# Last image of a four-layer network: layer 3's weights and position tables requested earlier, layer 2 in six PSUM banks, its result kept in SBUF

## The chip, the cores and the metric

The kernel runs on one core of one Trainium2 chip as one program for four images. The metric is device microseconds of that core. TensorE (PE) multiplies matrices, and its weight loads are listed apart (PEld); VectorE (DVE), ScalarE (ACT) and GpSimd (POOL) compute; SyncE (SP) issues nearly all DMAs, one after the other. Each engine takes its instructions in a fixed order: one that waits holds up all behind it.

## What is computed

The input is 4 images of 64x64 pixels (4096 tokens) with 128 channels, in float32. Each image passes through four layers:

```python
x = input + out_proj(norm(selective_scan(conv(in_proj(LN(input))))) * silu(z))   # layer 0
x = x + mlp(LN(x))
x = gamma * softmax_attention_over_all_tokens(x) + x                            # layer 1
y = hs(bn(conv1x1(x)))                                                          # layer 2, hs = hard swish
for m in range(2):
    y = y + hs(bn(conv3x3(hs(bn(conv1x1(y))))))
x = hs(bn(conv1x1(leaky(bn(concat(conv1x1(y), conv1x1(x)))))))
x = x + proj(softmax(q @ k + bias, over a 7x7 neighbourhood) @ v)               # layer 3, of LN(x)
x = x + mlp(LN(x))
```

In layer 3 a query sees 49 keys, and each of four heads adds a learned bias that depends on the offset between query and key.

## The kernel before

**Stages.** The selective scan of layer 0 takes most of the span: GpSimd, VectorE and ScalarE work on it without a break for images 0, 1, 2, 3 in turn. The rest of an image, `rest` (L1668), runs beside the next image's scan: `scan_output` (L581, layer 0's gate, projection and MLP), `layer1` (L731), `layer2` (L917) and `layer3_attention` (L1252). A tile scheduler orders each engine's instructions by priorities and estimated times, puts in the semaphore waits, and gives SBUF and PSUM space to pools as they open and close. A pool that takes space which another has held waits for that pool's last reader. So a load written early in the code can be issued only when its space is free, and one that is written late can be issued early.

The last image (3) has no scan beside it. For it `rest` is called with `scan_over` (L1747), which closes the scan's pools and so frees their SBUF, and the flag `wide` gives some stages larger tiles and more banks. When the scan ends, image 2's layer 3 is still at work; then comes image 3's `scan_output`, which steps image 2's last MLP beside it, and then layers 1, 2 and 3 of image 3.

**Tokens** are worked on in 8 chunks of 512 (8 rows). `transposed` keeps the image as xT, 128 channels by 4096 tokens, in SBUF from `scan_output` to the end of layer 2.

**Layer 2** first loads 15 small weights (`load`, through `loader`, L163, and L937 to L942); `norms` has the scales and shifts that the first activation (L956) reads. Then four kinds of phase follow: cv1 for all chunks; twice (m = 0, 1) the 1x1 convolutions of all chunks into `sides` tiles (two per step, with rows shifted by one for the next phase), and the 3x3 convolutions, twelve matmuls per chunk; at the end, chunk by chunk, cv3, cv2p and cv4 (L1003 to L1024). `hard_swish` (L952) is two activations on ACT and one or two operations on DVE. All PSUM tiles come from one pool of one-bank tiles, 8 for the last image and 4 for the others. The result `out_r` (L1021) of each chunk is stored to DRAM (x4).

**Layer 3.** `layer3_attention` loads its weights (12 loads for the last image, with those of the MLP), makes a bias row with a small matmul, and then works on chunks. `make_chunk` (L1328) loads the 512 tokens of a chunk from x4, normalizes and transposes them (`layernorm_T`, L178) and makes q, k and v, one chunk ahead of use. A chunk's keys are packed in four groups. `scores` (L1347) makes a group's scores, on the last image for all four heads at once (128x2048), takes the exp on ACT (L1361, tile e) and multiplies it on DVE by the exp of the bias (L1363). `products` (L1396) adds up the values and the denominators; `finish` (L1379) divides, projects and adds the residual, and on the last image queues the chunk's MLP, of which one step runs after each of the groups 1 to 3 of later chunks.

**Tables.** The biases lie in DRAM as tables by kind: 0 for chunk 0, 1 for chunks 1 to 6, 2 for chunk 7, four groups each. On the last image a table is 128x4x512 float32, 1 MB, loaded at its first use (`table`, L1318) and turned into its exp by ACT in place (L1324); twelve buffers hold all twelve. On images 0 to 2 tables are half as large, 8 buffers, and TensorE adds them to the scores (L1351) with no exp of their own.

Of the kernel before, what the change touches and what calls it, by code (L numbers as in the profile page):

```python
# [28 lines left out]
F32 = mybir.dt.float32  # L29
# [3 lines left out]
PSUM = bass.MemoryType.PSUM  # L33
# [880 lines left out]
    nc.sync.dma_start(D.w2_bias, last[0:1, 1, :])  # L914


def layer2(tc, K, A, D, img, xT, wide):  # L917

# [1 line left out]
    with ExitStack() as ctx:  # L922
        big = ctx.enter_context(tc.tile_pool(name="l2_big", bufs=1))
        pool = ctx.enter_context(tc.tile_pool(name="l2_w", bufs=2))
        psum = ctx.enter_context(tc.tile_pool(name="l2_ps", bufs=8 if wide else 4, space=PSUM))
        load = loader(tc, big, A, 2)
        cv1, cv2p = load("cv1_w", [128, 64]), load("cv2p_w", [128, 64])
        cv3 = big.tile([128, 64], F32, name="w2_cv3")
# [74 lines left out]
        for c in range(NCH):  # L1003
            i = c // (NCH // 2)
            half = slice(64 * i, 64 * i + 64)
            first = 1 + RC * c - i * (H - HALF)
            ps = psum.tile([128, LC], F32, name="ps")
            nc.tensor.matmul(ps[0:64, :], cv3[half, :], flat(y[half, first : first + RC, :]), start=True, stop=True)
            nc.tensor.matmul(ps[64:128, :], cv2p, xT[:, span(c)], start=True, stop=True)
            t = pool.tile([128, LC], F32, name="cat")  # L1010
            nc.scalar.activation(t, ps, AF.Identity, bias=norms[:, 5, 1:2], scale=norms[:, 5, 0:1])
            nc.scalar.activation(ps, ps, AF.Identity, bias=norms[:, 5, 1:2], scale=norms[:, 5, 0:1])
            nc.vector.scalar_tensor_tensor(t, t, 0.1, ps, ALU.mult, ALU.max)
            po = psum.tile([128, 4, 128], F32, name="ps")
            nc.tensor.matmul(
                po.rearrange("p t c -> p (t c)"), K.ones[0:1, :], bias.rearrange("p t c -> p (t c)"),
                start=True, stop=False,
            )
            for q in range(4):
                nc.tensor.matmul(po[:, q, :], t[:, span(q, 128)], cv4, start=False, stop=(q == 3))  # L1020
            r = pool.tile([128, 4, 128], F32, name="out_r")  # L1021
            nc.scalar.activation(r, po, AF.Relu, bias=K.half, scale=1.0 / 6.0)
            nc.vector.scalar_tensor_tensor(r, r, 1.0, po, ALU.min, ALU.mult)
            nc.sync.dma_start(token_tiles(D.x4[img], c), r)  # L1024

# [221 lines left out]
                nc.sync.dma_start(out[key_kind(c)][i], bt.rearrange("p h r w -> p h (r w)"))  # L1249


def layer3_attention(tc, K, A, D, img, wide, out=None):  # L1252

    nc = tc.nc
    NP = 4 if wide else 2
    with ExitStack() as ctx:  # L1260
        wpool = ctx.enter_context(tc.tile_pool(name="l3_w", bufs=1))
        pool = ctx.enter_context(tc.tile_pool(name="l3", bufs=2))
        psum = ctx.enter_context(tc.tile_pool(name="l3_p", bufs=1, space=PSUM))
        load = loader(tc, wpool, A, 3)
        n_w, n_b = load("norm1_g", [128, 1]), load("norm1_b", [128, 1])
        qkv, qkv_b, proj = load("qkv_w", [128, 3 * C]), load("qkv_b", [128, 3]), load("proj_w", [128, C])
        proj_b = load("proj_b", [1, C])
        qb = wpool.tile([128, 1], F32, name="qb")
        nc.vector.tensor_scalar_mul(qb, qkv_b[:, 0:1], HD**-0.5)


        made_in = ctx.enter_context(tc.tile_pool(name="l3_pm", bufs=1, space=PSUM)) if wide else psum

        def fresh(shape):
            return made_in.tile(list(shape), F32, name="fresh", tag="ps")


        pb = fresh((1, C))
        nc.tensor.matmul(pb, qkv_b[:, 2:3], proj, start=True, stop=True)
        bias = wpool.tile([1, 4, C], F32, name="bias_row")  # L1280
        nc.vector.tensor_add(bias, mid(pb, 4), mid(proj_b, 4))
        xs, qs, ks, vs, tables = {}, {}, {}, {}, {}
        mlps = []
        if wide:
            n2_w, n2_b = load("norm2_g", [128, 1]), load("norm2_b", [128, 1])
            P, together = load_mlp(load), Together(tc, K)

        def mlp_steps(c, x):
            xnT = pool.tile([128, LC], F32, name="xnT2", bufs=1)
            layernorm_T(tc, K, pool, made_in, x, n2_w, n2_b, xnT)  # L1290
            yield
            hT = pool.tile([128, NF, LC], F32, name="mlp_h", bufs=1)
            ph = psum.tile([128, NF, LC], F32, name="pair", tag="ps")
            for f in range(NF):
                mm = nc.tensor.matmul(ph[:, f, :], P.w1[:, span(f, 128)], xnT, start=True, stop=True)  # L1295
                if f == 0:
                    together.open(mm)
            together.run(
                mm,
                [  # L1300
                    lambda f=f: nc.scalar.activation(hT[:, f, :], ph[:, f, :], AF.Gelu, bias=P.b1[:, f : f + 1])  # L1301
                    for f in range(NF)
                ],
            )
            yield
            po = fresh((128, LC))
            for f in range(NF):
                nc.tensor.matmul(po, P.w2[:, f, :], hT[:, f, :], start=(f == 0), stop=(f == NF - 1))  # L1308
            yT = pool.tile([128, LC], F32, name="yT", bufs=1)
            nc.scalar.activation(yT, po, AF.Identity, bias=P.b2)  # L1310
            pt = fresh((128, 4, 128))
            for t in range(4):
                nc.tensor.transpose(pt[:, t, :], yT[:, span(t, 128)], K.ident)  # L1313
            nc.vector.tensor_add(x, x, pt)  # L1314
            nc.sync.dma_start(token_tiles(out, c), x)
            yield

        def table(c, i, p):  # L1318
            kind = key_kind(c)
            if (kind, i, p) not in tables:  # L1320
                t = pool.tile([128, NP, LC], F32, name="table", bufs=12 if wide else 8)
                nc.sync.dma_start(t, D.biasT[kind][i][:, NP * p : NP * p + NP, :])
                if wide:
                    nc.scalar.activation(t, t, AF.Exp)  # L1324
                tables[kind, i, p] = t
            return tables[kind, i, p]

        def make_chunk(c):  # L1328
            x = pool.tile([128, 4, 128], F32, name="x", bufs=6 if wide else 2)
            nc.sync.dma_start(x, token_tiles(D.x4[img], c))  # L1330
            xs[c] = x
            xn = pool.tile([128, LC], F32, name="xnT", bufs=1)
            layernorm_T(tc, K, pool, made_in, x, n_w, n_b, xn)
            ps = fresh((128, 2, LC))
            for i in range(2):
                nc.tensor.matmul(ps[:, i, :], qkv[:, span(i, C)], xn, start=True, stop=True)
            qs[c] = pool.tile([128, LC], F32, name="q")
            nc.scalar.activation(qs[c], ps[:, 0, :], AF.Identity, bias=qb, scale=HD**-0.5)
            ks[c] = pool.tile([128, LC], F32, name="k", bufs=3)
            nc.scalar.activation(ks[c], ps[:, 1, :], AF.Identity, bias=qkv_b[:, 1:2])  # L1340
            ps = fresh((128, 4, 128))
            for t in range(4):
                nc.tensor.matmul(ps[:, t, :], xn[:, span(t, 128)], qkv[:, 2 * C :], start=True, stop=True)
            vs[c] = pool.tile([128, 4, 128], F32, name="v", bufs=3)
            nc.scalar.copy(vs[c], ps)

        def scores(c, i, p, group):  # L1347
            ps, t = psum.tile([128, NP, LC], F32, name="pair", tag="ps"), table(c, i, p)
            if not wide:
                for u in range(NP):  # L1350
                    nc.tensor.matmul(ps[:, u, :], K.ident, t[:, u, :], start=True, stop=False)  # L1351
# [11 lines left out]
                made = nc.vector.tensor_mul(e, e, t)  # L1363
            return [e[:, u, :] for u in range(NP)], made

        row = bias.rearrange("p t c -> p (t c)")

        def product(out, tile_, q0, q1, at, values, es, made, last):
            for h in range(HEADS):
# [9 lines left out]
        def finish(c, po, den):  # L1379
# [5 lines left out]
            pj = psum.tile([128, 4, 128], F32, name="pj", tag="den")  # L1385
            nc.tensor.matmul(pj.rearrange("p t c -> p (t c)"), K.ones[0:1, :], row, start=True, stop=False)
            for t in range(4):
                nc.tensor.matmul(pj[:, t, :], oT[:, span(t, 128)], proj, start=False, stop=(t == 3))
            x = xs.pop(c)
            nc.vector.tensor_add(x, x, pj)  # L1390
            if wide:
# [276 lines left out]
def rest(tc, K, A, D, img, last, scan_over=None, out=None):  # L1668


    wide = scan_over is not None
    with ExitStack() as ctx:
        xT = transposed(ctx, tc)
        scan_output(tc, K, A, D, img, xT, last, scan_over)
        layer1(tc, K, A, D, img, xT, wide)
        layer2(tc, K, A, D, img, xT, wide)
    layer3_attention(tc, K, A, D, img, wide, out)


def everything_again(tc, K, A, D, out):  # L1680
# [3 lines left out]
    for img in range(B):  # L1684
        with ExitStack() as ctx:
            S = make_scan(ctx, tc, K, A)
            scan_inputs(tc, K, A, D, img)
            selective_scan(tc, K, S, D, img)
        with ExitStack() as ctx:
            xT = transposed(ctx, tc)  # L1690
            scan_output(tc, K, A, D, img, xT, None)
            layer1(tc, K, A, D, img, xT, False)
            layer2(tc, K, A, D, img, xT, False)
        layer3_shifted(tc, K, A, D, img)
        layer3_mlp_alone(tc, K, A, D, img, out[img], 4)

# [135 lines left out]
```

## Time and profile before

| | us |
|---|---|
| median of 4 runs (8837.91 to 8844.23) | 8842.63 |
| the profiled execution | 8850.58 |
| its span, first to last instruction | 8848.8 |
| scan's end, last y_sum (ACT) | 7656 |
| image 3: first matmuls of layer 1 | 8044.6 |
| layer 1's last update of xT (DVE, end) | 8425.2 |
| first layer-2 weight load issued; `norms` issued; first activation (L956) | 8420.8; 8429.7; 8431.6 |
| last out_r activation of layer 2 | 8529.0 |
| layer 3: weight loads issued (12) | 8529.1 to 8534.7 |
| layer 3: tables issued (12) | 8536.2 to 8561.6 |
| layer 3: first exp of scores; the next | 8573.6; 8579.6 |

Busy shares over the span: PE 80%, DVE 81%, ACT 64%, POOL 80%. The profile cuts the span in 40 slices of 221 us and gives each engine's busy share in tenths; the last image's layers fill the slices from 36 on. A windows view gives, for any stretch, each engine's busy time with its instruction count, the TensorE clock that was granted (PEclk, 1.00 is full speed), the share of the DMA engines' time and the rate in GB/s. A timeline view lists one engine's instructions: start, duration, operation and tiles, and in brackets the idle time before and what ended it.

### The profile page before, as it was taken

To read this page: it belongs to the slowest core of one execution; us is meant where nothing else is said; L and a number is where in the kernel's file an instruction comes from. 1 tells how busy PE (TensorE), PEld (TensorE's weight loads), DVE (VectorE), ACT (ScalarE), POOL (GpSimd) and SP (SyncE) were. 2 spreads that over 40 slices of the span, in tenths; PEclk is the share of its full clock that TensorE was granted. 3 is DMA by queue.
4 is the path that set the end of the run, shared out by engine and by line. 5 is a ranking of instruction groups with operands and counts; after the bars stand their busy time and mean duration, and the time that the engine had idled before them with its cause. 6 is when DMAs were issued, how large, how long until landed. Compare 5 with 4: busy or idle time off the path is not lost. (4 is left out here: it accounts for less than half of the span.)

```text
span 8848.8 us, 102218 instructions
## 1 busy us (share of the span) xinstructions
PE 7045.3 (80%) x30532; PEld 2633.4 (30%) x30532; DVE 7136.6 (81%) x8531; ACT 5686.2 (64%) x11661; POOL 7046.6 (80%) x3079
## 2 busy tenths in 40 slices
PE   6845858687788888787789888777799987788988
PEld 2211313132332222233322222334322222344333
DVE  4788978787999999997899999988899999513433
ACT  5646767676676676666766676667766676454356
POOL 6888999989899998997799999998899989500000
PEclk8756868797789998888899998888899988899989
DMA  5777676777545456565454556665455565320020
GB/s 186 243 231 242 238 252 239 261 242 266 192 162 170 168 173 216 194 210 185 164 168 166 182 168 227 201 216 182 157 173 172 176 214 196 107 71 6 1 81 12
DMA packets 855474, 1572.03 MB, mean 178 GB/s; under 512 B 218341, under 2 KB 336764, under 8 KB 851197
## 3 DMA queue, kind: packets, MB, share of 16 engines
q1 hardware_dynamic: 724605, 1389.21, 47.2%
q10 hardware_dynamic: 130304, 176.19, 5.6%
q8 instruction: 245, 4.01, 0.2%
q14 instruction: 320, 2.62, 0.1%
HBM read 1273.92 MB, written 280.18 MB: 176 GB/s over the span
## 5 line engine op out<-in xcount | busy, mean ns | idle before, releaser
L501 POOL TENSOR_TENSOR dB<-du,b_rows 128x1024 f32<-128x1024 f32 x2048 | 4813.7, 2384 | 490.4 <-issue 127.9
L507 ACT ACTIVATE dA<-dt,w_A_log 128x512 f32<-128x512 f32 x4096 | 2781.7, 690 | 504.9 <-DVE hc L509 239.8
L509 DVE TENSOR_TENSOR_SCAN dA<-dA,state,dB 128x512 f32<-128x512 f32 x2128 | 2631.6, 1273 | 275.0 <-POOL dB L501 139.3
L522 POOL TENSOR_TENSOR hc<-hc,c_rows 128x1024 f32<-128x1024 f32 x832 | 1984.4, 2385 | 46.0 <-ACT state L518 21.5
L509 DVE TENSOR_TENSOR_SCAN hc<-dA,state,dB 128x512 f32<-128x512 f32 x1456 | 1801.9, 1268 | 186.3 <-ACT dA L507 106.3
L514 DVE TENSOR_TENSOR hc<-dA,c_rows 128x512 f32<-128x512 f32 x2432 | 1564.8, 676 | 79.1 <-PE py L555 64.3
L555 PE MATMUL py<-hc,pick 128*32 128x512 f32 x8192 | 1251.3, 685 | 403.7 <-POOL hc L522 310.1
L516 ACT COPY state<-dA 128x1 f32<-128x1 f32 x2128 | 326.7, 159 | 1299.5 <-DVE hc L514 1292.8
L845 PE MATMUL pa<-e,l_v 128*128 128x512 f32 x2048 | 1062.0, 650 | 26.5 <-ACT e L801 25.2
L797 PE MATMUL pair<-l_g,l_f 32*128 32x512 f32 x2048 | 529.3, 663 | 163.9 <-ACT e L801 119.9
L801 ACT ACTIVATE e<-pair 128x1024 f32<-128x1024 f32 (+1 forms) x448 | 508.4, 1135 | 232.1 <-PE pair L797 224.2
L985 POOL MEMSET l_h<- 64x128 f32 x8 | 1.7, 212 | 815.0 <-DVE l_h L959 815.0
L845 PEld LDWEIGHTS pa<-e,l_v 128*128 128x128 f32 x2048 | 374.6, 199 | 677.9 <-issue 615.1
L555 PEld LDWEIGHTS py<-hc,pick 128*32 128x32 f32 x8192 | 210.3, 116 | 1171.8 <-POOL hc L522 461.7
L247 PE MATMUL ps<-band,w_conv_diag 128*128 128x504 f32 (+3 forms) x1152 | 500.8, 594 | 7.6 <-ACT delta L397 7.2
L1351 PE MATMUL pair<-table,ident 128*128 128x512 f32 x768 | 405.6, 653 | 103.9 <-ACT e L1361 79.9
L509 DVE TENSOR_TENSOR_SCAN dA<-dA,dB 128x512 f32<-128x512 f32 x304 | 356.2, 1213 | 63.5 <-POOL dB L501 55.3
L201 PE MATMUL ps<-ident,ln_xn 128*128 128x128 f32 x512 | 143.6, 374 | 307.4 <-ACT ln_xn L198 239.4
L328 POOL TENSOR_TENSOR du<-delta,xc 128x1024 f32<-128x1024 f32 x128 | 332.7, 2606 | 53.4 <-ACT delta L397 46.7
L1361 ACT ACTIVATE e<-pair 128x1024 f32<-128x1024 f32 (+1 forms) x224 | 254.7, 1137 | 174.5 <-PE pair L1355 174.2
L247 PEld LDWEIGHTS ps<-band,w_conv_diag 128*128 128x128 f32 x1152 | 221.4, 193 | 285.5 <-issue 264.5
L797 PEld LDWEIGHTS pair<-l_g,l_f 32*128 32x128 f32 x2048 | 139.6, 188 | 517.7 <-ACT e L801 255.5
(285 smaller groups left out, 8739.8 us busy)
## 6 DMA issues: line engine op xcount, KB each, us to landing
b_rows<-bc_dram SPq DMA_DIRECT2D x1024, 256.0 KB
c_rows<-bc_dram SPq DMA_DIRECT2D x1024, 256.0 KB
dt<-delta_dram SPq DMA_DIRECT2D x512, 512.0 KB
du<-du_dram SPq DMA_DIRECT2D x512, 512.0 KB
delta_dram<-delta ACTq DMA_DIRECT2D x128, 512.0 KB
du_dram<-du SPq DMA_DIRECT2D x128, 512.0 KB
table<-biasT_dram SPq DMA_DIRECT2D x72, 512.0 KB
y_first_dram<-y_sum ACTq DMA_DIRECT2D x128, 256.0 KB
```

Of the source, the lines that this page charges most:

```text
L247: mm = nc.tensor.matmul(out[:, r0 - row0 : r1 - row0, c0:c1], lhsT((dy + 1) * 3 + dx + 1), src[:, r0 + dy : r1 + dy, c0 + dx : c1 + dx], s ...
L328: nc.gpsimd.tensor_mul(du.rearrange("p d (a b) -> p d a b", b=H), deltas[b].rearrange("p d (a b) -> p d a b", b=H), tk,)
L501: nc.gpsimd.tensor_mul(dB, dus[pp], mid(bt, 2))
L507: nc.scalar.activation(dA, dts[pp][:, g, :], AF.Exp, scale=S.A[:, k, j, pr, g : g + 1])
L509: nc.vector.tensor_tensor_scan(hg[:, order], dA[:, order], dB[:, g, order], 0.0 if i == 0 else state[:, j, pr, g : g + 1], ALU.mult, ALU.add,)
L514: mm = nc.vector.tensor_mul(hc[:, g, :], dA, ct)
L522: made.append(nc.gpsimd.tensor_mul(hc, hc, mid(ct, 2)))
L555: mm = nc.tensor.matmul(py[0][32 * q : 32 * q + 32, :], S.pick, hcs[q // 2][:, q % 2, :], start=(k == 1 and j == 0), stop=(j == NJS - 1),)
L797: nc.tensor.matmul(ps[:, u, :], f[quad, t // 4, span(t % 4, 128)], g[quad, c, :], start=True, stop=True)
L801: made = nc.scalar.activation(e, ps, AF.Exp)
L845: nc.tensor.matmul(pa, v[:, 8 * q + t, :], es[q], start=(t == 0 and q == 0), stop=(t == 7 and q == 3),)
L1351: nc.tensor.matmul(ps[:, u, :], K.ident, t[:, u, :], start=True, stop=False)
```

## The change

Images 0 to 2 keep their code path. For image 3:

- `layer3_early`, called between `scan_output` and `layer1`, opens the pool of layer 3's weights, writes their 12 loads, and opens a pool `l3_t` for tables and tokens.
- `layer3_made`, called between `layer1` and `layer2`, writes the loads and exps of the eight tables of kinds 0 and 1, and opens the pool in which chunks are made (`l3_m`) and its two PSUM banks (`l3_pm`), which stay open through layer 2; it also makes the bias row.
- Tables have 8 buffers in place of 12. Those of kind 2 are loaded where chunk 7 asks for them, into the buffers of kind 0; the scheduler may issue them as soon as those are free.
- `layer2` has 6 PSUM banks in place of 8, and its eight out_r tiles (8 buffers, 256 KB each, in `l3_t`) become layer 3's tokens `xs[c]`. They are neither stored to x4 nor loaded again.
- `layer3_attention` uses what has been made; `make_chunk` starts with the layernorm.

The core of the diff (the renaming of `n_w` to `L3.n_w` and the like is left out):

```diff
@@ layer2
-        psum = ctx.enter_context(tc.tile_pool(name="l2_ps", bufs=8 if wide else 4, space=PSUM))
+        psum = ctx.enter_context(tc.tile_pool(name="l2_ps", bufs=6 if early else 4, space=PSUM))
...
-            r = pool.tile([128, 4, 128], F32, name="out_r")
+            r = (early.tokens if early else pool).tile([128, 4, 128], F32, name="out_r", bufs=NCH if early else 2)
...
-            nc.sync.dma_start(token_tiles(D.x4[img], c), r)
+            if early:
+                early.xs[c] = r
+            else:
+                nc.sync.dma_start(token_tiles(D.x4[img], c), r)
@@ new
+def layer3_table(tc, D, L3, NP, c, i, p):
+    kind = key_kind(c)
+    if (kind, i, p) not in L3.tables:
+        t = L3.tokens.tile([128, NP, LC], F32, name="table", bufs=8)
+        tc.nc.sync.dma_start(t, D.biasT[kind][i][:, NP * p : NP * p + NP, :])
+        if NP == 4:
+            tc.nc.scalar.activation(t, t, AF.Exp)
+        L3.tables[kind, i, p] = t
+    return L3.tables[kind, i, p]
+
+def layer3_early(ctx, tc, K, A):
+    wpool = ctx.enter_context(tc.tile_pool(name="l3_w", bufs=1))
+    L3 = layer3_weights(tc, K, A, wpool)
+    load = loader(tc, wpool, A, 3)
+    L3.n2_w, L3.n2_b = load("norm2_g", [128, 1]), load("norm2_b", [128, 1])
+    L3.P = load_mlp(load)
+    L3.tokens = ctx.enter_context(tc.tile_pool(name="l3_t", bufs=1))
+    return L3
+
+def layer3_made(ctx, tc, K, D, L3):
+    for c in range(2):
+        for i in range(4):
+            layer3_table(tc, D, L3, 4, c, i, 0)
+    L3.made = ctx.enter_context(tc.tile_pool(name="l3_m", bufs=2))
+    L3.made_in = ctx.enter_context(tc.tile_pool(name="l3_pm", bufs=1, space=PSUM))
+    bias_row(tc, L3, L3.made_in.tile([1, C], F32, name="fresh", tag="ps"))
@@ make_chunk
-            x = pool.tile([128, 4, 128], F32, name="x", bufs=6 if wide else 2)
-            nc.sync.dma_start(x, token_tiles(D.x4[img], c))
-            xs[c] = x
+            if not wide:
+                xs[c] = pool.tile([128, 4, 128], F32, name="x")
+                nc.sync.dma_start(xs[c], token_tiles(D.x4[img], c))
@@ rest
-        layer1(tc, K, A, D, img, xT, wide)
-        layer2(tc, K, A, D, img, xT, wide)
-    layer3_attention(tc, K, A, D, img, wide, out)
+            if wide:
+                early = layer3_early(later, tc, K, A)
+            layer1(tc, K, A, D, img, xT, wide)
+            if wide:
+                layer3_made(later, tc, K, D, early)
+            layer2(tc, K, A, D, img, xT, early)
+        layer3_attention(tc, K, A, D, img, early, out)
```

## Prediction

> **What bounds the kernel now.** I read the busy table first: over the whole span VectorE, GpSimd and TensorE each work about 80%, but that is an average over stages, and the change touches only the last image, after the scan. So I went to the slices. GpSimd, which feeds the scan, is at 0 in the last five of 40; in the DMA row one slice there stands out, and it is where the granted TensorE clock dips again.
>
> ```profile
> POOL 6888999989899998997799999998899989500000
> PEclk8756868797789998888899998888899988899989
> DMA  5777676777545456565454556665455565320020
> ```
>
> Each slice is 221 us; slice 39 (8406 to 8627) holds the border between layers 2 and 3 of the last image. The windows around it show the hole (columns: PE, PEld, DVE, ACT, POOL busy, clock, DMA share, GB/s):
>
> ```profile
> 8470.00:8530.00 60.00, 57.79 (x236) 22.25 (x235) 21.65 (x34) 31.48 (x49) 0.31 (x2) 0.97 0.10 30
> 8530.00:8545.00 15.00, 2.41 (x7) 0.75 (x6) 3.45 (x19) 3.48 (x14) 0.00 (x0) 0.57 0.84 256
> 8545.00:8575.00 30.00, 16.03 (x49) 8.27 (x49) 1.15 (x8) 29.02 (x39) 0.00 (x0) 0.59 0.97 382
> ```
>
> Before 8530 TensorE sets the pace (57.8 of 60). Then for 13 us nothing computes: layer 3 waits for the stored result of layer 2 to come back, with its weights. From 8545 to 8575 ScalarE is full (29.0 of 30), because the exps of ten tables stand in its order ahead of the first exp of scores. One table costs, and so does its product:
>
> ```profile
> L1363 DVE TENSOR_TENSOR e<-e,table x32: 2291/2292/2294, 8575.5 to 8812.3; 128x2048 f32<-128x2048 f32 x32
> L1324 ACT ACTIVATE table<-table x12: 1893/1900/1917, 8544.3 to 8577.8; 128x2048 f32<-128x2048 f32 x12
> ```
>
> Last layer-2 result (ACT, L1022) at 8529.03, first exp of scores at 8573.56: 44.5 us. That is all there is to win. For the moved parts I used the built order of the changed kernel, instruction by instruction, which differs from what the diff suggests.
>
> **A. The eight early tables (+6.2).** They are not made in layers 1 and 2. Their SBUF is the scan's; in the built order SP issues the twelve layer-3 weights and eight 1 MB tables as soon as the scan ends (7658), and the eight exps stand in ScalarE's order between the exps of scores of image 2's layer 3:
>
> ```profile
> 7663.28 1.02 ACT L1361 ACTIVATE e<-pair 128x1024 f32<-128x1024 f32 x1 [3.82 <-PE pair L1355]
> 7667.51 1.02 ACT L1361 ACTIVATE e<-pair 128x1024 f32<-128x1024 f32 x1 [3.20 <-PE pair L1355]
> 7672.40 1.02 ACT L1361 ACTIVATE e<-pair 128x1024 f32<-128x1024 f32 x1 [3.87 <-PE pair L1355]
> 7676.63 1.02 ACT L1361 ACTIVATE e<-pair 128x1024 f32<-128x1024 f32 x1 [3.21 <-PE pair L1355]
> 7681.47 1.02 ACT L1361 ACTIVATE e<-pair 128x1024 f32<-128x1024 f32 x1 [3.82 <-PE pair L1355]
> ```
>
> After these five stand 1, 2, 3, 2 and 0 table exps. ScalarE waits 3.2 to 3.9 us for TensorE between them, so the 1.90 us of one exp would hide, and of three (5.7 us) 2 us would not. But the tables must have landed. In the trace of before, twelve of them completed 2.46 us apart. Twelve weight issues (5.5 us there) and 1.8 us to the first packet put table k (0 to 7) at about 7668.5 + 2.47k, the last at 7685.8; its exp ends at 7687.7, and the e that stood at 7681.47 is 6.2 us late. TensorE needs that e (it is busy 8.9 of 10 us there), nothing else runs beside it, and the stage has no later slack that I found. Bounds: 2.5 if all land early; 22 if they move at the 235 GB/s of the window 8535 to 8540 (below). Work is only added here, so no end lies below nothing.
>
> **B. Layer 1's start (+0.8).** Its four weights now wait for the last result of the stage before it, and land about 8045.3; its first work stood at 8044.6. Bounds 0 and 2.
>
> **C. Layer 2's weights (+4.45).** The scheduler gives them space that layer 1's pool holds, so 15 loads wait for layer 1's last update (8425.2) and not for 8420.8. Layer 2's first activation already waits for one of them:
>
> ```profile
> ACT hs_r L956 <- DMA w_norms<-w_norms_dram: 9.2, 1, 9.2
> ```
>
> It started at 8431.60 and would start at 8436.05. All of ScalarE's layer 2 stands behind it. Bounds 0 and 6.
>
> **D. Six banks for eight (+4.9).** While the 1x1 convolutions run, ScalarE takes two activations per tile, 1.22 us. The first 3x3 tile takes the bank of a tile two later than before: 2.45 us, twice. The 3x3 phase is TensorE's (4.77 us a chunk), so it isn't made up. Bounds 0 and 10.
>
> **E. The border (-35.2, net of C and D -25.8).** In the built order the layernorm, q, k and v of chunks 0 and 1 lie in layer 2's last phase. After the last out_r (ends 8529.7): v 0.58, xnT 0.76, q/k matmuls 1.9 (half of the 3.78 that four took at clock 0.5), q and k 1.25, v matmuls and scores 1.1, v 0.58: 8536.0. Ahead of it TensorE gets 4.3 us of new work (transposes 0.66 twice, q/k 1.9, v 1.04); the phase has some waits on DVE and ACT, so I count 2.4 (bounds 0 and 4.3): first e at 8538.4. With C and D 8547.7, against 8573.56. The x4 stores and loads of 2 MB each vanish with it. Bounds 21 and 31, with D, the widest of its parts, at its two ends.
>
> **F. The last chunk's four tables (+13.3).** They are kind 2, and their buffers are those of kind 0: each load waits for the product with the old table. The exps nevertheless stand in chunk 0, in the order e0, xnT, t0, e1, e2, t1, e3, q, k, t2, t3, e4. So ScalarE, in order, waits for: e0 1.9, product 2.3, first packet 1.8, 1 MB 2.46, exp 1.9: e1 10.2 us after e0. Before:
>
> ```profile
> 8573.56 1.87 ACT L1361 ACTIVATE e<-pair 128x2048 f32<-128x2048 f32 x1
> 8575.31 0.78 ACT L202 ACTIVATE xnT<-ps,w_norm_b,w_norm_g 128x512 f32<-128x512 f32 x1
> 8575.98 3.71 ACT L1324 ACTIVATE table<-table 128x2048 f32<-128x2048 f32 x2
> 8579.58 1.88 ACT L1361 ACTIVATE e<-pair 128x2048 f32<-128x2048 f32 x1
> ```
>
> 6.0 us. By the same steps e3 stands at 20.4 (before 13.4; t1 lands 4.3 after e1's product), and e4 at 30.4 (before 17.1), behind t3, whose buffer frees with e3's product. Loss 13.3. TensorE and DVE wait for these e's; nothing covers it. Bounds 8 (part regained in the wait for chunk 0's end) and 18.
>
> The clock: in the 13 us hole it fell to 0.50 and matmuls took twice as long until 8575; the change removes that hole and sets waits of about 5 us into F. [...] Our trace shows only the longer hole. [...]
>
> **Sum.** +6.2 +0.8 -25.8 +13.3 = -5.5 us. The profiled execution took 8850.6 (span 8848.8 and 1.8 around it), 8 us above the median 8842.6 of the runs shown; I take the change off the median: **8837**. Best and worst bounds together: -31+2.5+0+8 = -20.5; -21+15+2+18 = +14 (15 for A: half the tables at the slow rate). So 8822 to 8857 if this case holds.
>
> [...]
>
> **Rivals.**
> 1. *The border is won and F is covered* (faster, 0.25). If the e's of chunk 0 come late but chunk 1 and the MLP that follow have the slack (before, e5 to e6 took 13.6 us, much of it waits), the 13.3 come back. -25.8+6.2+0.8 = -18.8; with A at 2.5, -22.5: about 8821. For it: the last chunks end on TensorE, not on ScalarE. Against it: TensorE is busy 29.6 of 35 us right after, so it has little slack to regain with.
> 2. *The tables move slowly* (slower, 0.13). Place: SP's queue at 7658 and in chunk 0. With p us per MB, A is 8p - 13.6 and F 13.3 + 3(p - 2.46). The total is zero at p = 3.0 and passes +17.7 at p = 4.6. At 4.46 (235 GB/s) it is about +16, and with E at its low end of 21 it is +21: 8859 to 8864. For it: image 2's own store and load stand behind the tables on SP. Against it: nothing else uses the queues then (10 GB/s).
> 3. *The change moves no end* (no change): A and F eat E. That is my forecast, 0.62 with its size.
>
> 0.2% (17.7 us) is about what a measurement of this kernel can tell from no change. Of the forecast's 0.62, 0.03 lies on the faster side of that and 0.01 on the slower. Faster 0.28, same 0.58, slower 0.14. The range takes in rival 1 with some 7 us below it, and the forecast's upper bound: 8814 to 8858.
>
> **What would show it.** Right: ScalarE's e's at 7663 to 7688 with table exps between, waiting for DMA; layer 2 starting some 4 us later after layer 1; no hole at its end; chunk 0 taking some 13 us longer from e0 to e4, with table exps that wait for DMA. Wrong: e4 close to 17 us after e0 (rival 1), or table landings over 3 us apart at 7668 (rival 2); or the first e not 35 us, less C and D, nearer to layer 1's end.

## The result, and the profile after

The changed kernel takes 8852.87 us in the median (8836.81 to 8864.29, 40 runs) beside 8844.39 for the kernel before (60 runs): a ratio of 1.0009, 95% interval 1.0005 to 1.0013, some 8 us slower. I had forecast 5.5 us less. The time lies inside the range and within 0.2%, but the sign is wrong.

Whole times don't show where it is lost, and they scatter: the scan's end alone lies anywhere from 7642 to 7655 us in the profiles of this study, with the same scan. So every time below is counted **from the scan's end**, the start of its last y_sum on ScalarE (7655.48 before, 7649.32 after). The kernel's end then stands at 1193.3 before and 1204.1 after: +10.8.

| stage (us) | before | after | difference | forecast |
|---|---|---|---|---|
| scan's end to layer 1's first matmul (A, B) | 389.1 | 402.8 | +13.7 | +7.0 |
| layer 1, to its last update of xT | 380.6 | 380.8 | +0.2 | 0 |
| to layer 2's first activation (C) | 6.4 | 11.8 | +5.4 | +4.45 |
| to layer 2's last hard swish (D) | 62.8 | 71.7 | +8.9 | +4.9 |
| to its last out_r (last phase) | 34.7 | 34.2 | -0.5 | +2.4 |
| to the first exp of scores (E) | 44.5 | 9.0 | -35.5 | -37.5 |
| to chunk 1's first exp (F) | 17.0 | 32.6 | +15.6 | +13.3 |
| to chunk 1's last exp | 29.3 | 31.2 | +1.9 | 0 |
| to the end | 228.9 | 230.0 | +1.1 | 0 |
| sum | 1193.3 | 1204.1 | +10.8 | -5.5 |

The page's DMA row shows the move as a whole: the 2 of slice 39 is gone, and slice 35, with the scan's end, has a 4 instead of a 3.

```profile
DMA  5677677777554556565445556565445565420000
```

ScalarE's timeline of image 2's layer 3, after (start, duration, idle before and what ended it):

```profile
7657.12 1.02 ACT L1401 ACTIVATE e<-pair 128x1024 f32<-128x1024 f32 x1 [3.82 <-PE pair L1395]
7665.81 1.91 ACT L1283 ACTIVATE table<-table 128x2048 f32<-128x2048 f32 x1 [7.66 <-DMA table<-biasT_dram]
7667.62 1.01 ACT L1401 ACTIVATE e<-pair 128x1024 f32<-128x1024 f32 x1
7668.53 3.94 ACT L1283 ACTIVATE table<-table 128x2048 f32<-128x2048 f32 x2
7673.62 1.02 ACT L1401 ACTIVATE e<-pair 128x1024 f32<-128x1024 f32 x1 [1.16 <-PE pair L1395]
7674.55 5.50 ACT L1283 ACTIVATE table<-table 128x2048 f32<-128x2048 f32 x3
7679.94 1.01 ACT L1401 ACTIVATE e<-pair 128x1024 f32<-128x1024 f32 x1
7680.85 1.91 ACT L1283 ACTIVATE table<-table 128x2048 f32<-128x2048 f32 x1
7684.26 1.91 ACT L1283 ACTIVATE table<-table 128x2048 f32<-128x2048 f32 x1 [1.50 <-DMA table<-biasT_dram]
7686.07 1.01 ACT L1401 ACTIVATE e<-pair 128x1024 f32<-128x1024 f32 x1
```

The exps stand where the built order had them. The first waits 7.66 us for its table, and the scores behind it wait too: the e at 26.0 before stands at 36.8. The windows there:

```profile
7655.00:7660.00 5.00, 3.88 (x15) 1.54 (x13) 0.15 (x1) 1.02 (x1) 0.00 (x0) 1.00 0.69 143
7660.00:7665.00 5.00, 3.17 (x41) 1.62 (x40) 0.00 (x0) 0.00 (x0) 0.00 (x0) 1.00 0.90 320
7665.00:7670.00 5.00, 1.32 (x2) 0.81 (x3) 0.00 (x0) 4.19 (x3) 0.00 (x0) 0.56 1.02 429
7690.00:7700.00 10.00, 5.96 (x24) 2.51 (x16) 1.37 (x2) 1.23 (x2) 0.00 (x0) 0.50 0.11 32
```

The weights were issued from 7652.3, the first table at 7657.7. While the weights' transfers run (7655 to 7660) the DMA engines move 143 GB/s at 0.69 of their time; the tables' 429 GB/s comes only after. And TensorE, waiting, falls towards half clock (0.56 from 7665 to 7670). The 0.50 from 7690 on, around the end of image 2's first chunk, is no new thing as such: before the change the clock fell behind that chunk's end too (before):

```profile
7690.00:7700.00 10.00, 2.56 (x5) 1.23 (x6) 1.15 (x8) 3.87 (x12) 0.00 (x0) 0.50 0.12 33
```

Layer 2's start, in ScalarE's waits, and windows of its first and second 1x1 phase and of its end:

```profile
ACT hs_r L956 <- DMA w_norms<-w_norms_dram: 14.6, 1, 14.6
```

```profile
8450.00:8460.00 10.00, 10.00 (x34) 2.51 (x32) 5.15 (x9) 10.00 (x18) 0.20 (x1) 0.50 0.00 0
8484.00:8496.00 12.00, 10.62 (x40) 2.69 (x38) 6.71 (x11) 12.00 (x20) 0.20 (x1) 0.72 0.01 2
8530.00:8570.00 40.00, 32.95 (x178) 16.03 (x176) 12.38 (x29) 27.76 (x59) 0.00 (x0) 1.00 0.08 27
```

The wait for `norms` grew from 9.2 to 14.6. In the 1x1 phases the clock is 0.50 and 0.72. From 8530 to 8570, over the border, TensorE works 33 of 40 us at full clock: the hole is gone. What follows it, ScalarE in layer 3's chunk 0 (its exps of scores and of tables alone):

```profile
8559.58 1.88 ACT L1401 ACTIVATE e<-pair 128x2048 f32<-128x2048 f32 x1
...
8568.58 1.91 ACT L1283 ACTIVATE table<-table 128x2048 f32<-128x2048 f32 x1 [6.46 <-DMA table<-biasT_dram]
8570.39 1.86 ACT L1401 ACTIVATE e<-pair 128x2048 f32<-128x2048 f32 x1
8574.46 1.88 ACT L1401 ACTIVATE e<-pair 128x2048 f32<-128x2048 f32 x1 [2.21 <-PE pair L1395]
8579.49 1.91 ACT L1283 ACTIVATE table<-table 128x2048 f32<-128x2048 f32 x1 [3.15 <-DMA table<-biasT_dram]
8581.31 1.86 ACT L1401 ACTIVATE e<-pair 128x2048 f32<-128x2048 f32 x1
...
8585.22 1.91 ACT L1283 ACTIVATE table<-table 128x2048 f32<-128x2048 f32 x1 [0.89 <-DMA table<-biasT_dram]
8590.39 1.91 ACT L1283 ACTIVATE table<-table 128x2048 f32<-128x2048 f32 x1 [3.26 <-DMA table<-biasT_dram]
8592.21 1.86 ACT L1401 ACTIVATE e<-pair 128x2048 f32<-128x2048 f32 x1
```

Four times ScalarE stops for a table that chunk 7 needs 200 us later, 13.8 us in all, and with the exps themselves chunk 0 takes 32.6 us instead of 17.0.

### The profile page after: what moved, and what is told of

The parts are those of the page before. It is cut to its first block, busy times and chain, and to the rows that moved or that the text cites. A ratio compares the mean times of both kernels' runs of the same rounds, so it can differ in the third digit from the quotient of the medians.

```text
span 8853.4 us, 102196 instructions
## 1 busy us (share of the span) xinstructions
PE 7063.4 (80%) x30532; PEld 2636.7 (30%) x30532; DVE 7137.3 (81%) x8531; ACT 5689.0 (64%) x11661; POOL 7047.9 (80%) x3079
## 5 line engine op out<-in xcount | busy, mean ns | idle before, releaser
L522 POOL TENSOR_TENSOR hc<-hc,c_rows 128x1024 f32<-128x1024 f32 x832 | 2022.3, 2431 | 49.7 <-ACT state L518 22.1
```

The costliest lines, as they stand in the source:

```text
L522: made.append(nc.gpsimd.tensor_mul(hc, hc, mid(ct, 2)))
```

## The experiments

My theory: the border is won as forecast, and four things take it back, each through an engine that takes its instructions in order and waits: A (early tables), F (last tables), C (layer 2's weights), D (banks). The rivals are told run by run. The first six runs undo one thing each; the later ones put the cures together and take parts of the gain away again.

In the table below stages are as above; "A+B" is the time to layer 1's first matmul. Layer 1 and the stages behind chunk 0 are left out, so a row doesn't add up to its end. The stages and the end are those of one profiled execution for each kernel; the median and the ratio are of all its runs. Each ratio is to runs of the kernel before taken beside it, whose medians are 8844.4 to 8849.3.

| run | A+B | to layer 2's first act. | hard swishes | last phase | border | chunk 0 | end | median us | ratio to before (interval) |
|---|---|---|---|---|---|---|---|---|---|
| before | 389.1 | 6.4 | 62.8 | 34.7 | 44.5 | 17.0 | 1193.3 | 8844.4 | 1 |
| the change | 402.8 | 11.8 | 71.7 | 34.2 | 9.0 | 32.6 | 1204.1 | 8852.9 | 1.0009 (1.0005 to 1.0013) |
| loads and exps later | 392.1 | 11.6 | 71.7 | 34.2 | 8.9 | 38.9 | 1204.2 | 8849.8 | 1.0005 (0.9995 to 1.0014) |
| exps later | 389.1 | 10.7 | 72.5 | 34.2 | 8.9 | 38.5 | 1194.0 | 8849.3 | 1.0007 (0.9997 to 1.0016) |
| last tables later | 402.7 | 11.4 | 72.0 | 34.2 | 9.0 | 15.4 | 1185.7 | 8838.0 | 0.9993 (0.9984 to 1.0003) |
| layer 2's weights early | 399.7 | 2.5 | 72.8 | 34.3 | 8.9 | 45.1 | 1206.6 | 8860.1 | 1.0019 (1.0009 to 1.0029) |
| banks 8, then 6 | 399.2 | 11.1 | 62.8 | 54.0 | 8.9 | 32.6 | 1207.0 | 8860.2 | 1.0016 (1.0006 to 1.0025) |
| layer 3's weights later | 392.6 | 11.5 | 71.9 | 34.2 | 9.0 | 36.8 | 1197.4 | 8852.3 | 1.0010 (1.0000 to 1.0019) |
| **three edits** | 389.1 | 2.5 | 70.5 | 34.3 | 8.9 | 17.8 | 1159.8 | **8816.6** | **0.9969 (0.9957 to 0.9980)** |
| four edits | 389.4 | 1.7 | 64.7 | 54.0 | 9.0 | 15.4 | 1177.0 | 8818.6 | 0.9968 (0.9956 to 0.9980) |
| four, bias row first | 392.6 | 3.2 | 63.4 | 56.9 | 9.0 | 15.4 | 1185.8 | 8828.0 | 0.9979 (0.9970 to 0.9988) |
| three, tokens by DRAM | 388.6 | 2.5 | 72.8 | 38.2 | 11.7 | 15.4 | 1166.6 | 8820.2 | 0.9975 (0.9965 to 0.9984) |
| three, eight banks | 389.2 | 2.0 | 64.5 | 33.9 | 18.5 | 15.5 | 1161.6 | 8820.6 | 0.9973 (0.9963 to 0.9983) |
| three, tables at the border | 389.2 | 1.8 | 72.0 | 34.2 | 11.7 | 25.0 | 1173.5 | 8832.0 | 0.9979 (0.9969 to 0.9989) |

Chunk 0's column moves with edits that have nothing to do with it (32.6 to 45.1 among runs that keep the last tables there): the scheduler puts the four table exps at slightly different places in ScalarE's order each time (after e0, e2 and twice after e3 in the changed kernel; after e0, e1, e2 and e3 where it takes 45.1), and each place costs another wait. That is why stages are compared, not ends. Other stages move by some us, too, where no edit touches them: layer 1, with the same eight exps in it, takes 377.8 us with three edits and 384.3 with four. With one profile for each kernel, differences of that size prove nothing.

**Early tables later (A).** `marks` holds layer 1's exps.

```diff
 layer3_made
-            layer3_table(tc, D, L3, 4, c, i, 0)
+            layer3_table(tc, D, L3, 4, c, i, 0, marks[0, 4], marks[2 + (4 * c + i) // 2, 4 * (i % 2)])
 layer3_table(..., load_after=None, exp_after=None)
+        after(tc, got, load_after)      # the load waits for that instruction
+            after(tc, exp, exp_after)   # and so does the exp
```

> The changed kernel with one thing moved: the loads of the eight early tables wait for an exp of layer 1's chunk 0, and their exps for exps of chunks 2 to 5, two per chunk. Theory (ScalarE takes its instructions in order, so the scores of image 2's layer 3 waited behind table exps whose 8 MB had not landed): image 2's layer 3 ends 126.9 us after the scan's end as before, not 140.5, and layer 1 starts at about 389, not 402.8. The exps hide in layer 1, where ScalarE idles 2.8 us ahead of each exp of scores. The whole kernel is 12 to 14 us faster than the changed one: about 8840. Rival (the twelve weight loads or TensorE's lower clock cost that time, or the exps disturb layer 1 as much): 5 us or less gained, 8848 to 8853.

Image 2's layer 3 ends at 126.8, as the theory said; yet the whole gained nothing that its interval can tell. Layer 1 started at 392.1 instead of 389.1 and took 384.9 instead of 380.8, and chunk 0 took another 6.3 us. So image 2's stage speaks for the theory, and the end for the rival.

**Only the exps later.** The first argument above is None: the loads stay at the scan's end.

> The changed kernel with its loads of the eight early tables where they were (at the scan's end), but their exps in layer 1, after exps of chunks 2 to 5. Theory (the in-order wait of ScalarE is the cost, not the traffic): as the run with both moved, image 2's layer 3 ends near 127 us after the scan's end, the whole at about 8840. Rival (the 8 MB hold up image 2's own transfers, which stand behind them on SP and in the DMA engines): at least half of the 13.6 us stays, layer 1 starts at 396 or later, 8846 or more.

ScalarE's timeline at the same place:

```profile
7654.78 1.02 ACT L1408 ACTIVATE e<-pair 128x1024 f32<-128x1024 f32 x1 [3.82 <-PE pair L1402]
7659.00 1.02 ACT L1408 ACTIVATE e<-pair 128x1024 f32<-128x1024 f32 x1 [3.20 <-PE pair L1402]
7663.90 1.02 ACT L1408 ACTIVATE e<-pair 128x1024 f32<-128x1024 f32 x1 [3.87 <-PE pair L1402]
7668.13 1.02 ACT L1408 ACTIVATE e<-pair 128x1024 f32<-128x1024 f32 x1 [3.21 <-PE pair L1402]
7672.97 1.02 ACT L1408 ACTIVATE e<-pair 128x1024 f32<-128x1024 f32 x1 [3.82 <-PE pair L1402]
```

To the hundredth these are the gaps of before, with 8 MB moving beside them (windows of the same stretch):

```profile
7660.00:7665.00 5.00, 3.88 (x33) 1.76 (x25) 0.00 (x0) 1.05 (x2) 0.00 (x0) 1.00 0.99 418
7665.00:7670.00 5.00, 5.00 (x45) 2.31 (x46) 0.00 (x0) 1.02 (x1) 0.00 (x0) 1.00 1.01 426
```

Layer 1 starts at 389.1 and takes 380.7, with eight exps in it. So the cost of A was ScalarE's order, not the traffic; the rival falls. Image 2's layer 3 ended at 129.8, though, not near 127: its second chunk came 2.9 us late, when the tables had landed. With three edits, whose loads stand at the same place, it ended at 126.7. At the first exp of scores the run is 14.1 us ahead of the changed kernel (896.2 beside 910.3); chunk 0 gives 6 of them back. Its median (8849.3 for 8852.9) doesn't show the 10 us of the profile's end; the interval of ten runs is 17 us wide. That layer 1 was 4 us longer in the run before this one is not shown to come from the loads inside it: with four edits, whose loads stand at the scan's end, it took as long.

**The last chunk's tables later (F).** `seen` holds layer 3's exps of scores.

```diff
 scores
-            ... layer3_table(tc, D, L3, NP, c, i, p)
+            ... layer3_table(tc, D, L3, NP, c, i, p, L3.seen.get((3, i)), L3.seen.get((4, i)))
```

> The changed kernel with the last chunk's four tables loaded after the exps of layer 3's chunk 3 and turned into their exps after those of chunk 4. Theory (chunk 0 is slow because four table exps stand in ScalarE's order, each waiting for a product and a 1 MB load): from the first exp of scores to the fifth 17 us as before, not 32.6, and chunk 1 regains its order: 15 to 20 us faster than the changed kernel, 8833 to 8838. Rival (TensorE or DVE sets chunk 0's pace once its tokens come without a gap, so that the tables only filled idle time): the fifth exp at 25 us or later and less than 8 us gained. A second rival: the four exps cost as much in chunk 4 (7.6 us of ScalarE).

The fifth exp comes 15.4 us after the first. The end is 18.4 us earlier, with layer 1 starting where it did (402.7): F is worth 18, of which 17.2 stand in chunk 0. Theory held, both rivals fell: chunk 4, which has the table exps now, takes 34.5 us to chunk 5's first exp where the changed kernel took 31.3, and chunk 5 then 30.3 where it took 31.3, so some 2 us come back and not 7.6.

**Layer 2's weights early (C).** The 15 loads move into a function and a pool on xT's side, opened ahead of layer 1.

```diff
 rest
+                pool2 = ctx.enter_context(tc.tile_pool(name="l2_early", bufs=1, side="right"))
+                weights = layer2_weights(tc, A, D, pool2)
             layer1(tc, K, A, D, img, xT, wide)
```

> The changed kernel with layer 2's 15 weight loads in a pool of their own, opened before layer 1 in space that the layer-0 stage has held. Theory (the weights wait for layer 1's space, and TensorE's clock falls to 0.5 in the wait, which slows the first 1x1 phase): layer 2's first activation comes 2 to 5 us after layer 1's last update of xT, not 11.8; the granted clock in the first 1x1 phase is over 0.8; 8 to 11 us faster than the changed kernel, about 8843. Rival (only the wait for the weights counts; the clock costs nothing, since ScalarE paces that phase): 5 to 7 us faster, about 8847.

Layer 2 starts 2.5 us after layer 1, not 11.8: the wait for the weights is all that was won, 9.3 us. The part on the clock fell: the 1x1 phase ran at 0.68, 1.00 and 0.51 in windows of 5 us (8430 to 8445), and the hard swishes took 72.8. So with six banks the clock falls there with early weights too. As a whole this run is one of the two slowest (8860.1; the theory had 8843, the rival 8847), for its chunk 0 took 45.1 us.

**Eight banks for the convolutions (D).**

```diff
 layer2
-        psum = ...tile_pool(name="l2_ps", bufs=6 if early else 4, space=PSUM)
+        psum = convs.enter_context(tc.tile_pool(name="l2_ps", bufs=8 if early else 4, space=PSUM))
 ... ahead of the last phase
+            convs.close()
+            early.open()    # l3_pm and the bias row
+            psum = ctx.enter_context(tc.tile_pool(name="l2_ps6", bufs=6, space=PSUM))
```

> The changed kernel with layer 2's convolutions in eight PSUM banks again; the last phase (cv3, cv2p, cv4) has six, and layer 3's two banks are opened between. Times from the scan's end in the profile, as image 2's tables move everything behind them. Theory (six banks starve TensorE in the 1x1 phases; it starts the 3x3 phase late and at half clock): from the first to the last hard-swish activation 63 us as before, not 71.7, and the first exp of scores still about 9 us after the last out_r, so 8 to 9 us come off the time from layer 2's start to layer 3's first exp. Rival (the 9 us come from the late weights and the cold clock at layer 2's start, not from the banks): 68 us or more stay. The whole: 8844 to 8850 by the theory if layer 3's chunk 0 keeps its order, which the scheduler may change.

62.8 us, to the tenth as before, though layer 2's weights are nearly as late as in the changed kernel: D is the banks', and the rival falls. The clock belongs to it: from 8450 to 8460, in the first 1x1 phase, it is 0.91 here, and 0.50 in the same window of the changed kernel (above), whose 1x1 phase starts within 0.3 us of this one.

```profile
8450.00:8460.00 10.00, 9.16 (x52) 3.03 (x44) 5.14 (x9) 10.00 (x17) 0.20 (x1) 0.91 0.00 0
```

But the last phase took 54.0 us instead of 34.2, and so the whole 8860.2, not 8844 to 8850. The same is seen in the run with four edits, below.

**Layer 3's weights out of the tables' way.** The twelve loads are gated by `marks[0, 4]`; tables and exps stay.

> The changed kernel with layer 3's twelve weight loads moved into layer 1 (they wait for an exp of its chunk 0), the eight early tables and their exps as they were. Theory (my term for the early tables was too small because the weights' small packets stood ahead of them in the DMA queues and cost some 4 us beside the 5.5 us of issuing them): the first table lands some 6 us after the scan's end, not 16.5, the last at some 25, not 35; image 2's first chunk ends (its reciprocal) at 30 to 34 us, not 41.5, and layer 1 starts at 391 to 396, not 402.8. Rival (the 8 MB and TensorE's clock cost the time by themselves, wherever they start): layer 1 starts at 399 or later.

The first table exp starts 8.0 us after the scan's end (16.5 before this edit), image 2's first chunk ends at 35.3 and layer 1 starts at 392.6: 10.2 of the 13.7 us were the weights ahead of the tables. The theory held for layer 1's start and the rival fell; the first landing and the chunk's end came 2 and 1 us later than it had them. Beside what is left stands the clock: after ScalarE's first wait of 4 us TensorE works at half clock for 10 us. How much of the 3.5 us it makes, no run separates.

```profile
7650.00:7655.00 5.00, 3.42 (x32) 1.60 (x24) 0.00 (x0) 1.38 (x1) 0.00 (x0) 1.00 0.92 385
7655.00:7665.00 10.00, 8.50 (x36) 3.54 (x40) 0.00 (x0) 7.71 (x6) 0.00 (x0) 0.51 1.01 426
7665.00:7680.00 15.00, 12.69 (x97) 5.61 (x92) 0.00 (x0) 10.42 (x8) 0.00 (x0) 0.99 0.34 139
```

**Three edits together**: exps later, last tables later, layer 2's weights early.

> Three of the earlier edits together on the changed kernel: exps of the early tables in layer 1, the last chunk's tables in chunks 3 and 4, layer 2's weights in a pool of their own. If the three losses are independent, the end comes 1204 - 10 to 14 - 16 to 18 - 8 to 9 = 1163 to 1170 us after the scan's end (before: 1193), some 25 us under the kernel before: ratio 0.9965 to 0.9975. If they cover one another (a loss upstream hides one downstream), at most half of that: 0.998 or more.

1159.8, a little under the range, and 8816.6 us: the losses add up, as they do when they are independent, and a version faster than the kernel before comes out, by 0.31% (0.20 to 0.43). 3.0 us of the gain are layer 1's, where no loss was expected to go.

**Four edits**: the three, and eight banks for the convolutions.

> The same three and eight banks for layer 2's convolutions. If the banks cost what the trace of the changed kernel shows (9 us from the first to the last hard swish), the end comes at 1154 to 1162 us after the scan's end, some 30 to 38 us under the kernel before: ratio 0.9957 to 0.9966. If TensorE's clock at the phases' starts was the cost, with or without banks: no better than the three alone.

A miss. The convolutions gained 6 us, and the last phase lost 20. The whole time doesn't repeat this: 8818.6 beside 8816.6 with three edits, six runs of each, though the profiles' ends lie 17 us apart. In the profile of four edits the scan ended 9.6 us earlier (7641.65 beside 7651.27); whether that is chance or belongs to the kernel stays open. The long last phase itself is seen in all three kernels that change banks there. TensorE at the change of banks, and windows before, in and after it:

```profile
8477.48 4.20 PE L1006 MATMUL ps<-l_h,w_taps 128*64 128x384 f32 x24
...
8484.26 0.59 PE L1286 MATMUL fresh<-w_proj_w,w_qkv_b 128*1 128x128 f32 x2 [2.58 <-DVE l_y L972]
8484.77 1.96 PE L1022 MATMUL ps<-l_y,w_cv 64*64 64x512 f32 x2
```

```profile
8470.00:8480.00 10.00, 10.00 (x56) 3.33 (x54) 2.94 (x6) 2.63 (x4) 0.00 (x0) 1.00 0.00 0
8485.00:8515.00 30.00, 30.00 (x44) 8.19 (x43) 6.80 (x23) 10.01 (x22) 0.00 (x0) 0.50 0.00 1
8520.00:8540.00 20.00, 19.20 (x88) 9.96 (x88) 6.50 (x14) 14.84 (x33) 0.00 (x0) 1.00 0.00 0
```

Behind a gap of 2.58 us the clock is 0.50 for 30 us, although TensorE is busy all the time: L1022's two matmuls take 1.96 us, which in the undisturbed phase take 1.07.

**The bias row first.** It is made ahead of layer 2 in a bank of its own.

> The kernel with all four edits, with layer 3's bias row made ahead of layer 2 in a PSUM bank of its own, so that the first TensorE instruction after the change of banks no longer waits for the last 3x3 tile's hard swish. In the run with four edits TensorE idled 2.6 us there, its clock fell to 0.50 and stayed so for 33 us, though TensorE was busy without a break: the last phase took 54 us instead of 34. Theory (that gap alone cost the 20 us): the gap is under 1 us, the clock stays 1.00, from the last hard swish to the last out_r 34 to 36 us, the end 1154 to 1158 us after the scan's end, the whole 8803 to 8812 and a ratio of 0.995 to 0.9965. Rival (the banks that the last phase takes over are freed late whatever comes first): the gap and the half clock stay, no better than four edits.

A miss, and as the rival had it: the gap is 2.58 us again, now ahead of L1022, which waits for the same hard swish, and the last phase takes 56.9 us. So in both runs the first instruction on the banks that change hands waits for their last reader, 2.58 us, be it the bias row's matmul or L1022's. That the gap makes the half clock is therefore not tested: no run took it away at this place.

**Tokens by DRAM again**, on the three edits.

```diff
-            r = (early.tokens if early else pool).tile(...)
+            r = pool.tile([128, 4, 128], F32, name="out_r", bufs=2)
+            nc.sync.dma_start(token_tiles(D.x4[img], c), r)
 make_chunk
+            xs[c] = L3.tokens.tile([128, 4, 128], F32, name="x", bufs=NCH if wide else 2)
+            nc.sync.dma_start(xs[c], token_tiles(D.x4[img], c))
```

> The kernel with three edits, but with out_r stored to DRAM and loaded again as layer 3's tokens, as before the change (weights and tables still early, six banks). This is what the kept tokens alone are worth. Theory (the store and load of 2 MB are most of what made the border long): from the last out_r to the first exp of scores 22 to 28 us, not 8.9, so 13 to 19 us slower than with three edits: about 8832. Rival (the late weights, the late tables and their ten exps ahead of the first scores made the border, and chunk 0's tokens are long in DRAM by then): under 14 us, at most 5 us slower.

The border is 11.7 us and the end 6.8 us later. The theory fell, and the rival's 5 us were passed by a little: keeping the tokens is worth about 7 us; 2.8 are lost at the border and 3.9 in the last phase.

**Eight banks to layer 2's end**, on the three edits; layer 3's two open after it, so its chunks are made after it.

> The kernel with three edits, but layer 2 has eight PSUM banks to its end and layer 3's two are opened after it; tables, weights and tokens as with three edits. It sets the price of six banks (8 to 9 us of layer 2) against what the two banks buy (chunks 0 and 1 made inside layer 2's last phase). Theory: from the first to the last hard swish 63 to 65 us, not 70.5; from the last out_r to the first exp of scores 14 to 20 us, not 8.9, since the transposes, q, k and v of chunk 0 at least come after it; a wash, the end 1156 to 1164 us after the scan's end, ratio 0.9965 to 0.998. Rival (the change of banks stops TensorE for over 2 us, and its clock falls to half for some 30 us, as in the runs that changed banks inside layer 2): chunks 0 and 1 run at half clock, the end at 1168 or later.

A wash, as expected: the convolutions gain 6.0, the border loses 9.6, chunk 0 gains 2.3; 1161.6 beside 1159.8. The clock dipped to 0.66 over 10 us only (8525 to 8535), so the rival's half clock of 30 us did not come.

**Tables at the border again**, on the three edits: loads gated by the last out_r activation.

> The kernel with three edits, but the eight tables of kinds 0 and 1 are requested only after layer 2's last out_r activation and turned into exps from there, so at the border as before the change; weights and tokens as with three edits. This is what making tables early is worth. Theory (ten table exps ahead of the first exp of scores made 30 us of the border before, so the tables are most of it): the first exp of scores stays near 9 us after the last out_r or comes some us later, but chunk 0 waits on ScalarE for tables again; chunk 1's first exp comes 15 to 25 us later than with three edits (905.0 us after the scan's end), the end near 1175 to 1185, the whole at about 8835. Rival (with weights and tokens there, the loads of 2.5 us each hide behind the chunk's own work of 3.6 us per group): 5 us or less, about 8821.

The end is 13.7 us later: 3.4 of it stand before the last out_r, which the tables don't touch, 2.8 at the border and 7.2 in chunk 0. So early tables are worth some 10 us: less than my theory's 15 to 25, more than the rival's 5.

## Why the prediction was wrong

**What held.** Nearly every step went the way it was put: the tables between image 2's exps, the late `norms`, the banks' price in both 1x1 phases, the hole gone, chunk 0 stopped by tables. The border's size was right: last phase and border together -36.0 measured, -35.2 forecast. Two errors met in that: the 2.4 us of new TensorE work cost nothing (the last phase took 0.5 us less), and the border itself gave 2.0 us less than its -37.5.

**A failed by size, and is the largest part of the error**: +13.7 with B where I had 7.0, 6.7 of the 16.3 us between forecast and profile (D 4.0, F 2.3, chunk 1's later groups 1.9). B cost only 0.2: TensorE idles 1.08 us ahead of layer 1's first matmul, where it idled 0.84. The step that failed was "twelve weight issues (5.5 us there) and 1.8 us to the first packet put table k (0 to 7) at about 7668.5 + 2.47k", 13.0 us after the scan's end for the first and 30.3 for the last. Their exps started at 16.5 and 34.9. Those 4.6 us at the last table are the whole error of the e behind it: 6.2 forecast and 4.6 make the 10.8 measured. I counted the issue of the weights and not their transfer (143 GB/s in that window), although the same loads stood ahead of the tables in the trace of before too. The other 2.7 us came behind that e, in image 2's next chunks, where I had put nothing. TensorE works at 0.50 there (7690 to 7700), and I had left the clock out of A and named it for F alone; but that the clock makes the 2.7 us is not shown.

**D failed by size**: 8.9 for 4.9. "The first 3x3 tile takes the bank of a tile two later than before: 2.45 us, twice" is seen: in both rounds the 3x3 matmuls start 2.9 us later after the first 1x1 matmul. Not counted: each 3x3 phase then starts at low clock (0.50 until 8460.9 in the first round, 0.60 from 8491 to 8496 in the second) and takes 1.3 us more in the first round and 1.8 in the second. Together that is the 8.9. Eight banks alone bring back 62.8.

**C** was 5.4 for 4.45, and **F** 15.6 for 13.3: a single load of 1 MB behind a product made ScalarE wait 6.5 us the first time. The clock, for which the sum has no term, did fall in F (0.51 from 8570 to 8577); how much of the 2.3 us is its, no run separates. F did not come back later (rival 1); undone, it gave 18.

**Of the rivals**, the second (slow tables) has the right place, and what happened lies below its price (up to +16 in all), but its condition fails: the tables came at 429 GB/s. They came late, not slowly. The terms (A up to 15, C to 6, D to 10, F to 18, the border net of C and D from 21) were all inside their bounds, but A, C, D and F all in the upper half and the border, at 21.7, almost at its end. The sum of them all, not one surprise, turned the sign. And 0.2%, which I took for about the least that a measurement here can tell, is too much: with 40 and 60 runs 0.09% stands clear of nothing (0.05 to 0.13).

**One reading fell short, without costing anything**: I wrote that "layer 3 waits for the stored result of layer 2 to come back, with its weights". The layernorm did wait for the tokens' load, but that load was requested only at 8535.2, behind the twelve issues of the weights from 8529.1 on. From 8539.6 on VectorE works on the layernorm, so nothing computes for 10 us rather than 13. Taken back one at a time from the three edits, the store and load are worth 7 us, the early tables some 10, and the chunks made inside layer 2 another 10 at the border (18.5 us without it, for 8.9). These three need not add up to the 36 us, and the weights were not tried alone.

## What to carry to other kernels

A load that is made early is not free by being early: ask in whose order its consumer stands. Here the eight loads cost nothing and the eight exps 13 us, because ScalarE took them in order between another stage's exps; the same exps some 480 us later were free (layer 1 took 380.7 us with them and 380.6 before). A scheduler that fills by estimated landing times needs a gate at such places, and a transfer that shares the queue belongs in the estimate with its bytes, not with its issue time (here twelve weight loads cost 8.5 us, of which their issue was 5.4). Where a stage's times scatter more than the change is worth, count stage by stage from an event in the profile, and try cures together: here three of them, none of which alone was clearly faster than the kernel before, together make 0.31% less.

## What I had not expected of the hardware

- TensorE's granted clock stayed at 0.50 for 30 us of uninterrupted matmuls after an idle gap of 2.58 us (four edits, 8485 to 8515). With the bias row first, after the same gap, L1022's pairs of matmuls took 1.93 to 1.97 us instead of 1.07 for 35 us (8494 to 8529). And the clock fell to 0.52 (8488 to 8492) in a 1x1 phase whose largest gap was 0.92 us (second round of the changed kernel): its last eight matmuls took 2.99 us. With three edits the same phase, with gaps of 0.91, 0.21, 0.26 and 0.26 us, took 0.97 us for each four of its last twelve matmuls, as before the change at 1.00. So in these runs the length of the gaps alone doesn't tell what the clock does.
- In the traces' record of the clock, before and after the change, every stretch at 0.50 or 1.00 except each trace's last one lasts a whole number of steps of 3.41 us (505 of 506 and 511 of 512 stretches). The kernel before, from 4.1 us ahead of the scan's end: 37.55 at 1.00, 13.65 at 0.50, 3.41 at 1.00, 3.41 at 0.50.
- Twelve weight loads ahead of the tables cost 8.5 us to the first table's exp (16.5 us after the scan's end with them ahead, 8.0 without), of which their issue was 5.4 (7652.3 to 7657.7).
- Eight 1 MB loads at some 420 GB/s beside a chunk of matmuls and exps cost it nothing: its gaps were those of the run without them to the hundredth of a microsecond.
